# A new order for the prologue and the first two blocks of a planned kernel

## The chip, the cores and the metric

The kernel runs on one core of one Trainium2 chip. A core has five engines, each with its own queue that runs in order: TensorE (PE in the profile; PEld is its loading of weights), VectorE (DVE), ScalarE (ACT), GpSimd (POOL) and SyncE (SP), which here only issues transfers. An engine waits for another through semaphores. The metric is the time on the device in microseconds (us), the median of several runs. The profile shows one execution, with each instruction's start and duration.

## The reference

The reference carries `x` (128 sequences of 64 tokens, 256 features, fp32) through four layers, each added to its input. In short:

```python
# L0: style-modulated self-attention; q = k = v, 16 heads of 16
style = s @ aff_w.T + aff_b                       # one per sequence
w_mod = w[None] * style[:, None, :]
demod = rsqrt(sum(w_mod * w_mod, axis=2) + 1e-8)
kx    = einsum('bni,boi->bno', x, w_mod * demod[:, :, None]) + b
A     = softmax(einsum('bnhd,bnjd->bnhj', kx, kx) / 4)
x    += modulated_linear(einsum('bnhj,bnjd->bnhd', A, kx), s, o_aff_w, o_aff_b, o_w, o_b)
# L1: bottleneck, its weights made from the conditions
x    += x + relu(x @ (down * (c @ dg) + c @ db)) @ (up * (c @ ug) + c @ ub)
# L2: h, t, s are layer norms of x with gain and bias from tables;
#     m, n, r are x plus a small MLP of one condition each
cat   = concat([w0*h, w1*t, w2*m, w3*n, w4*r, w5*s])      # w = softmax(aw)
x    += layernorm(silu(cat @ W1 + b1) @ W2 + b2)
# L3: a weight matrix of rank 30 per sequence, decoded from mu
U     = (mu @ W_dec + b_dec).reshape(B, 257, 30)
x    += x @ (U[:, :256] @ V) + U[:, 256] @ V
```

## The kernel before

The 8,192 tokens are 16 blocks of 512 (8 sequences), each in 4 tiles of 128 tokens. A prologue makes what all blocks share. `prologue_keys` loads the weights of the attention and makes the styles and their demodulation: `style` (L512 on), `square` on GpSimd (L527 for the style, L528 for the weights), a product (L463), `root` (L535 adds, L536 takes the square root on ScalarE), a reciprocal (L544, L575), a store of `demod_k` to memory. `prologue_rest` makes the conditions of the other layers: `dgdb` and `ugub` by products with the conditions, stored and loaded again for each block; the softmax of `aw` (`wsm`, L599 to L603, whose exponential is L600); the scaled `int_W1` (L613, L620; GpSimd adds three of its parts to `w_x`, L624 and L625); `gtab` and `beta`, split into three bf16 terms by `terms_of` (L487 casts, L489 subtracts) and copied into place by ScalarE (L635, L655, L660); three small MLPs (L691 to L760); and 16 products by `W_dec` (`by_k`, L807, with VectorE's L812 behind each), stored as `ud`.

`attention` loads a block's inputs, has GpSimd multiply `xT` by the style (L900) and make the bottleneck's weights (`wdn` L931 and L937, `wup` L944 and L945), runs `tile_attention` for each tile, and ends with the output product (L957). One tile's attention is a chain over four engines: keys (L990), times demodulation (VectorE, L998), plus bias (GpSimd, L1004), a transpose (L1015), a copy `kR` (ScalarE, L1023), scores into the one `sc` buffer of four PSUM banks (L1046), maxima (VectorE, L1055, two), a copy of `mt` (ScalarE, L1065), a transpose (L1071), `mX` (ScalarE, L1078), `mTb` (VectorE, L1085), the shift by the maxima (L1096), exponentials (ScalarE, L1110, two), the product with the values (L1120), a transpose and a division (L1132 to L1139), a last transpose (L1150, L1155). The next scores need `sc` free, so they wait for the exponentials. `rest` runs the other layers of a block: down and up (L1178, L1196), layer norms (L1246 to L1276), the large product of the third layer (`int1`, L1314, fp32), the second (L1345), and the rank-30 product (L1388, L1414).

No loop sets the order of all this. Each operation is recorded in a `Plan` with its engine, an assumed duration, what it reads and writes and the buffers it needs; `Plan.order` then places the operations one after another. At each step it works out, for every operation that could be next, when it could start by these costs, and among those of an engine that can start within 0.02 us of the first it takes the one with the lowest turn number. The turn numbers are a table, `TURNS`: one list for the prologue, one each for the first and second block, one for the middle blocks, and one each for the last two; each block adds 400. The result is emitted in that order (`manual_schedule`), so the costs and numbers are only in the order, not in the program. Buffers go to operations in the same order, so another order also gives other buffer numbers.

What the costs of `order` know: TensorE's speed by windows of 3.41 us (full if the window before was busy for at least the share `BUSY`, by the weight `full` of each operation, and half otherwise); a switch of its tiling mode; SP's at most 8 transfers under way; and for operations with `pair=True`, VectorE operations that can't run beside a GpSimd one: such an operation starts only once GpSimd is free, and GpSimd's next only once it ends (`locked`).

Of the kernel before, what the change touches and what calls it, by code (L numbers as in the profile page):

```python
# [58 lines left out]
class Plan:  # L59
# [8 lines left out]
    LAG, WINDOW, BUSY, SEEN = 0.04, 3.41333, 0.4, 0.2  # L68
    TRANSFERS = 8
    SWITCH, KEEP = 0.08, 20.0  # L70
# [7 lines left out]
    def op(self, eng, took, emit, reads=(), writes=(), busy=None, claims=(), full=0.0, mode=0, pair=False, dma=0.0):  # L78
# [3 lines left out]
        o = dict(eng=eng, took=took, busy=took if busy is None else busy, emit=emit, full=full, mode=mode, pair=pair, dma=dma)  # L82
# [34 lines left out]
    def order(self):  # L117
# [18 lines left out]
        at, self.cells, landed, mode, locked, moved = {}, {}, [], 0, 0.0, 0.0  # L136
        ready = [o for o in ops if not o["wait"]]
        done = []
        while ready:
            best = {}  # L140
            for o in ready:
                pe = o["eng"] == "PE"
                other = at.get("POOL", 0.0) if o["pair"] else locked if o["eng"] == "POOL" else 0.0
                t = max([other, at.get(o["eng"], 0.0)] + [ops[d]["end"] + lag for d in o["deps"]] + [ops[d]["start"] for d in o["turn"]])
                need = {}
                for b in o["new"]:
                    need[b.kind] = n = need.get(b.kind, 0) + 1
                    free = self.free[b.kind]
                    if len(free) < n or (b.kind != "bank" and queue[b.kind][n - 1] is not b):
                        t = None  # L150
                        break
                    t = max(t, free[n - 1][0])
                if t is not None:
                    turn = o["prio"] - (self.KEEP if pe and bool(o["mode"]) == bool(mode) else 0.0)
                    best.setdefault(o["eng"], []).append((t, turn, o["n"]))
# [14 lines left out]
            if o["pair"]:  # L170
                locked = t + busy
            end = t + busy
# [29 lines left out]
    71 -14398 -26219 -39789 -3508 -7530 -8445 29350 -4645 -39544 -3719 31372 -23989 30872 -14104 -5225 32197 -4221  # L202
    -20468 16613 -32877 -15653 -20126 -4305 17337 6437 13955 1211 8610 -23732 17461 -40912 -33335 -37982 18051 10261
    200 -21211 -22777 -22750 -19011 -31532 -38047 -18609 7721 -34432 31396 -30213 -679 15634 -39760 15949 -34699
    42222 -32162 15768 -5238 -5839 -20496 -39810 -12031 32129 13701 32628 -5022 1049 17854 -28441 32340 -37891 -34297
    40989 -25748 -28541 36465 -17679 38337 -22124 -6381 -37871 18397 -22278 -45484 359 -1911 -29323 -49300 -46805
    4635 -91 19167 -31700 -47713 -3381 -5076 -40598 19254 -40704 18632 -38248 -38002 -13488 31826 -1701 18828 3175
    -34947 -15633 30124 -16980 57 31764 -8724 -42612 -38724 16630 18116 -23340 -3254 34040 -6466 -9239 -17832 33055
    -23773 14566 13689 29338 -5407 10846 18282 -1510 -48233 -30581 18938 -9903 -31147 21661 -7420 14038 17055 -42955
    -24882 -44299 -21176 -726 -25186 -4651 20657 -3370 30678 -10954 -12642 16581 -41643 -10283 17089 16935 -34492  # L210
    -21043 16515 -11836 16306 474 20673 5948 20829 15096 -17378 -4570 -24029 -14861 -3069 -28510 -6908 11872 21266
    -7806 -33448 -4644 8056 15322 -42611 20277 36585 -44360 -16351 17707 851 14726 16244 -34751 18196 38165 4440
    -13853 24639 -7896 11150 -5 -23772 15865 -46146 -35855 8441 32138 18178 -4413 -26345 -20553 14288 -39700 -47007
    10030 -4358 -34041 21308 -35652 17392 39213 13899 33152 -32620 15142 6721 14013 -35072 -14537 -1097 36082 -8009
    15339 34551 -34485 -1237 16822 -28641 -995 -30869 21364 16878 -14817 8219 -40040
    """,
    "first": """
    17249 -4174 -37661 40560 -2686 40232 13607 -21165 15661 -35071 -20748 8523 15848 9653 39437 -5504 -23078 -1003
    -23922 -12775 15184 21386 -5436 -38182 19015 -15238 17414 -6091 -41343 -14156 -19323 20301 -28060 25276 -38410
    -2885 8514 30733 -41166 16152 18629 10031 -32415 13671 6709 10311 35215 25762 -47432 6628 -14459 2665 -14344  # L220
    33918 17006 30738 -26444 -13871 5063 17282 -34231 16470 15297 -28168 -35683 -38013 -31479 885 -7241 -1609 -4616
    -35314 15778 11985 18356 16765 -13012 18386 -3827 -16703 27973 -35935 10508 16756 5142 -46417 5504 18379 -43542
    -36657 7698 34702 18688 18600 -8539 -6552 -43063 -6405 17215 7670 17794 -46636 -20647 -18240 29788 13458 -50498
    17553 -40018 -5173 19673 -30267 14660 3213 -4518 -35471 16525 7438 21762 -27033 17454 5856 -22658 -2548 -42968
    -1045 15141 -34414 -39228 -14781 -32852 -43405 37326 31094 -38278 -35006 17883 9658 -37158 15564 -38868 7399
    -45467 -810 -3547 329 -32846 -31322 21073 4944 -15877 -38629 42680 21792 -34201 -21934 27191 -15901 20512 -13401
    16412 -37057 16322 -44377 16841 27701 -19654 -45211 14418 17982 1404 -41845 16978 -6419 33218 -47006 34193 -25681
    18315 -8335 16994 -28170 43 18629 -3156 20131 9477 21282 21307 32185 16991 15525 4535 -26810 -36671 -3596 1849
    -43739 5277 -26259 31830 2526 -32783 -8029 -38301 21067 -6295 32999 -2430 -21725 333 -34823 -20585 13688 -13143
    -172 -33364 17594 16389 33686 -21070 -29862 -1422 30891 -7582 17309 -38340 1077 5561 -35769 19468 32463 -4083  # L230
    -628 16680 29479 -48232 -5761 -41402 5650 -34631 -43613 -42339 10399 -31952 -32906 29668 15652 13515 20461 -49991
    33105 34993 -35357 13650 -3425 -35040 -6276 17773 17502 19908 -34232 19985 20667 17372 -33978 13863 17147 16170
    -5010
    """,
    "second": """
    15875 16149 -15780 27079 -20038 -41412 -8527 31339 40458 -26784 -39981 -34505 -38008 -375 36397 -39093 23481
    17340 -7441 -37170 -1220 15851 -26304 -20057 16484 -24298 -9079 -48163 33051 -20470 33180 18143 16005 38721
    -21353 -42755 -3614 -4788 14775 16964 -7134 18850 -4650 13895 -18457 -12127 -3196 15705 16609 -6918 17201 16712
    -32722 -43102 2125 -36980 -4604 -39251 -25222 14438 18190 -28048 -3836 34949 -9979 -4441 -32439 3107 15923 -39292
    -32927 -3558 24709 -39978 35894 -1987 10347 -16156 -14048 12123 -39989 -47288 -29542 -31213 17510 12771 -39522  # L240
    -24706 17103 -6414 16875 22486 15550 -17008 14260 -37972 31898 -26161 164 -3567 -5559 -3644 -11986 -15142 -37679
    -47068 -2565 112 -47293 -2329 -35624 -30772 -35416 1153 -49693 -39768 14735 14656 32941 -6653 17076 29341 14823
    36957 -25310 35672 11924 20229 -23521 563 -19103 -28734 15957 8197 -3347 -31953 -40558 14704 -29232 17459 31147
    13855 -21768 14747 -40363 -30781 17758 34423 -14900 18160 813 20332 -5502 -27118 20085 27410 -21398 -50590 -26
    -3284 -8181 -3096 17263 -5282 15919 2531 -24344 -17581 -25179 16905 17897 13804 16385 33415 6275 -35571 15524
    -42367 -21853 28842 -5521 -15908 11063 -46061 -32321 -28271 14599 -169 4650 -27658 -31994 16439 -21317 -15239
    -27657 20557 -15331 30644 15572 37274 17208 -12718 -33262 -37729 -35554 4024 -28730 -40544 -17618 20660 39655
    -40762 -1182 18506 51 15653 -15776 34385 -51216 14294 -4243 -3255 -1485 -4941 -15608 -15247 -16446 -39940 13494
    -21568 16893 -29157 -7041 1652 -1804 -32667 32525 -12963 17265 -13279 236 6378 -43363 13245 6986 -46750 -41386
    -14016 40622 19379 -6583 -2003 -41355 -20538 -9037 13996 -11722 19545 -25139 -14909 11788 5525 -6727 -14631 16271  # L250
    -15192 -29513 -22936 17714 29105
# [53 lines left out]
def resid_chain(ctx: ExitStack, tc: tile.TileContext, a: dict, out: bass.AP, nblk: int = NBLK):  # L305
# [129 lines left out]
    def act(n, f, reads, writes, more=0.0):  # L435
        us = 0.085 + n / 1200 + more
        op("ACT", us + 0.08, f, reads, writes, busy=us)
# [20 lines left out]
    def product(us, ps, rows, cols, terms, reads, claims=()):  # L458
# [6 lines left out]
        pe(us, f, reads, [ps], claims)  # L465
# [16 lines left out]
    def terms_of(x, rows):  # L482

        out = []
        for t in range(TERMS):
            y = Buf("pb")
            dve(F, lambda y=y: nc.vector.tensor_copy(y.t[:rows], x.t[:rows]), [x], [y])  # L487
            if t < TERMS - 1:
                dve(F, lambda y=y: nc.vector.tensor_tensor(x.t[:rows], x.t[:rows], y.t[:rows], ALU.subtract), [x, y], [x])  # L489
# [3 lines left out]
    def prologue_keys():  # L493
# [37 lines left out]
        def root(dst, ps, n, part=None):  # L531
# [4 lines left out]
            act(n, lambda: nc.scalar.activation(view(), view(), AF.Sqrt), [d], [d])  # L536
# [1015 lines left out]
```

## Time and profile before

| | us |
|---|---|
| median of 3 runs | 910.79 (910.15 to 916.7) |
| the profiled execution, its time | 915.64 |
| its span, first to last instruction | 913.9 |
| TensorE busy | 835.8 (91%) |
| VectorE busy | 635.7 (70%) |
| GpSimd busy | 608.3 (67%) |
| ScalarE busy | 452.0 (49%) |

The page cuts the span into 40 slices; a digit is the busy share in tenths, and the row PEclk is the clock that TensorE was granted. The mean granted clock over the span is 0.967. By stretches, from the windows:

| stretch, us | TensorE busy | VectorE | ScalarE | GpSimd | clock |
|---|---|---|---|---|---|
| 0 to 130 | 98.0 | 87.8 | 53.3 | 71.8 | 0.87 |
| 130 to 210 | 76.4 | 53.2 | 35.9 | 44.7 | 1.00 |
| 210 to 860 | 626.8 | 478.6 | 349.2 | 473.9 | 1.00 |
| 860 to 913.9 | 34.6 | 16.2 | 13.6 | 18.0 | 0.75 |

Work of the prologue runs among the first two blocks until about 125 us; a block in the middle takes some 47 us. Within the first 130 us TensorE waited longest for:

| TensorE's waiting line | for | us, times |
|---|---|---|
| L463 | the load of `early` | 9.9, 1 |
| L1071 | ScalarE's copy of `mt`, L1065 | 5.3, 3 |
| L1046 | ScalarE's exponentials, L1110 | 2.4, 2 |
| L1150 | ScalarE's copy of `beta`, L655 (a bank) | 1.9, 1 |
| L1096 | VectorE's `mTb`, L1085 | 1.5, 2 |
| L463 | GpSimd's square of the style, L527 | 1.4, 1 |

### The profile page before, as it was taken

What the parts mean: (1) busy time and instruction counts of PE and PEld (TensorE: products, weight loads), DVE (VectorE), ACT (ScalarE), POOL (GpSimd) and SP (SyncE); (2) the same over time, 40 slices, a digit from 0 to 9 for tenths busy, and PEclk for the clock granted to TensorE, in tenths of its full rate; (3) what the DMA queues carried; (4) which work ended last, traced back from release to release, by engine and by line L of the source; (5) the groups of instructions that cost most, each with busy time, mean ns of one, the idle gap of its engine ahead of it and who ended that gap; (6) DMA issues with size and microseconds to landing.
All of it is one profiled execution on the core that took longest, in us unless ns stands there. A gap on an engine that the chain in (4) does not pass through costs nothing.

```text
span 913.9 us, 23971 instructions
## 1 busy us (share of the span) xinstructions
PE 835.8 (91%) x9752; PEld 538.6 (59%) x9752; DVE 635.7 (70%) x1363; ACT 452.0 (49%) x827; POOL 608.3 (67%) x826
## 2 busy tenths in 40 slices
PE   4768989899999999999999999999999999999793
PEld 3546855656575665656665756566566656564432
DVE  2667876758687777768585868777776858585532
ACT  2543254646455554555564655545554546454321
POOL 5265580967869594959687795959595968754513
PEclk9778999999999999999999999999999999999986
DMA  8466770242324232233324232323323232101000
GB/s 274 112 177 184 240 233 25 68 126 72 104 81 127 75 97 90 74 114 91 117 83 117 70 114 80 120 65 91 105 82 114 82 95 82 48 17 56 13 12 24
DMA packets 62575, 90.24 MB, mean 99 GB/s; under 512 B 6328, under 2 KB 46200, under 8 KB 62464
## 3 DMA queue, kind: packets, MB, share of 16 engines
q1 hardware_dynamic: 57344, 71.92, 26.9%
q0 software_dynamic: 5120, 16.78, 5.8%
q8 instruction: 77, 1.26, 0.6%
q14 instruction: 34, 0.28, 0.1%
HBM read 75.44 MB, written 13.24 MB: 97 GB/s over the span
## 4 chain that ended last, share of the span: by engine, by line
PE 71%; DVE 9%; ACT 6%; POOL 3%; issue 2%; POOLq 0%; ACTq 0%; DVEq 0%
PE bank L1314 22%; PE sc L1046 7%; PE bank L1120 6%; PE bank L957 6%; PE bank L1345 5%; PE bank L990 5%; DVE mt L1055 3%; PE bank L1033 3%; PE sc L1096 2%; PE bank L1150 2%; PE bank L1290 2%; ACT uu L1284 2%; PE bank L1178 2%; PE bank L1196 2%; PE bank L1371 2%
## 5 line engine op out<-in xcount | busy, mean ns | idle before, releaser
L1110 ACT ACTIVATE e<-sc 128x1024 f32<-128x1024 f32 x128 | 126.0, 1023 | 81.7 <-PE sc L1096 79.2
L1055 DVE TENSOR_REDUCE mt<-sc 128x8 f32<-128x1024 f32 x128 | 151.7, 1205 | 18.5 <-PE sc L1046 18.4
L1139 POOL TENSOR_TENSOR att<-ao,rz 128x256 f32<-128x256 f32 x45 | 28.3, 628 | 72.7 <-DVE rz L1136 66.7
L1299 DVE TENSOR_TENSOR uu<-uu,bank 128x512 f32<-128x512 f32 x96 | 63.9, 680 | 13.9 <-PE bank L1290 13.0
L990 PE MATMUL bank<-wk,xsT 128*128 128x256 f32 x256 | 68.4, 400 | 0.7 <-POOL xsT L900 0.7
L1314 PE MATMUL bank<-uu,w_t 128*128 128x512 f32 x128 | 66.4, 627 | 2.1 <-DVE uu L1299 1.4
L1314 PE MATMUL bank<-uu,w_s 128*128 128x512 f32 x128 | 67.2, 607 | 0.0
L1004 POOL TENSOR_TENSOR kxe<-kxe,kbr 128x256 f32<-128x256 f32 x64 | 46.8, 730 | 27.3 <-DVE kxe L998 27.2
L1314 PE MATMUL bank<-x2T,w_x 128*128 128x512 f32 x128 | 64.5, 605 | 0.0
L453 POOL TENSOR_SCALAR ry<-mvy 128x4 f32<-128x4 f32 (+1 forms) x19 | 4.4, 232 | 88.1 <-DVE mvy L449 87.9
L1345 PE MATMUL bank<-w,uu 128*128 128x256 f32 x256 | 61.7, 384 | 1.0 <-DVE uu L1332 1.0
L957 PE MATMUL bank<-osT,wo 128*128 128x512 f32 x128 | 60.9, 617 | 0.8 <-DVE osT L1155 0.7
L1046 PE MATMUL sc<-kR,kT 24*128 24x128 f32 x1440 | 58.0, 291 | 2.6 <-ACT e L1110 2.6
L1314 PE MATMUL bank<-uu,w_h 128*128 128x512 f32 x128 | 59.0, 595 | 0.1
L1046 PEld LDWEIGHTS sc<-kR,kT 24*128 24x128 f32 x1440 | 49.2, 193 | 16.3 <-issue 5.7
L990 PEld LDWEIGHTS bank<-wk,xsT 128*128 128x128 f32 x256 | 47.7, 198 | 17.2 <-issue 10.3
L931 POOL TENSOR_TENSOR wdn<-gdb,late 128x512 f32<-128x512 f32 x32 | 40.7, 1276 | 25.1 <-PE bank L1178 23.8
L448 DVE BATCH_NORM_STATS2 st<-uu 128x6 f32<-128x256 f32 x119 | 48.7, 418 | 9.3 <-ACT uu L1249 5.8
L1345 PEld LDWEIGHTS bank<-w,uu 128*128 128x128 f32 x256 | 46.2, 190 | 8.6 <-DVE uu L1332 1.6
L1132 DVE STREAM_TRANSPOSE ao<-bank 128x512 f32<-128x512 f32 x45 | 32.1, 713 | 26.5 <-PE bank L1120 23.2
L1065 ACT COPY mt<-mt 128x16 f32<-128x16 f32 x64 | 13.1, 204 | 74.3 <-DVE mt L1055 71.9
L915 POOL DMA_INDIRECT pw<-in_pw,idx x39 | 40.1, 1028 | 7.8 <-issue 7.0
(195 smaller groups left out, 2089.4 us busy)
## 6 DMA issues: line engine op xcount, KB each, us to landing
xT<-in_xT SPq DMA_DIRECT2D x32, 256.0 KB
gdb<-dgdb SPq DMA_DIRECT2D x16, 512.0 KB
wup<-ugub SPq DMA_DIRECT2D x32, 256.0 KB
ubb<-ugub SPq DMA_DIRECT2D x32, 256.0 KB
dmk<-demod_k SPq DMA_DIRECT2D x30, 256.0 KB
out_x<-uu SPq DMA_DIRECT2D x35, 128.0 KB
ud<-uu SPq DMA_DIRECT2D x8, 512.0 KB
uT<-ud SPq DMA_DIRECT2D x16, 256.0 KB
```

What stands on the lines that cost most here:

```text
L448: dve(256, lambda: nc.vector.bn_stats(st.t, x.t), [x], [st])
L931: lambda w=w, dp=dp: nc.gpsimd.tensor_tensor(w(), gdb.t[:, :, 0:64], dp, ALU.mult),
L957: nc.tensor.matmul(ps.t, owT[:, c, bass.ts(oc, 128)], osT.t[:, c, :], start=(c == 0), stop=(c == C - 1))
L990: nc.tensor.matmul(ps.t[:, :F], xsT.t[:, c, bass.ts(tl, 128)], kwT[:, c, :], start=(c == 0), stop=(c == C - 1))
L1004: lambda: nc.gpsimd.tensor_tensor(kxe.t[:, :, 0:D], kxe.t[:, :, 0:D], heads(kinds["kbr"][0]), ALU.add),
L1046: nc.tensor.matmul(sc.t[:, q, bass.ts(g, 128)], of_g(kT.t)[r, g, :], of_g(kR.t)[r, g, :], start=(g == 0), stop=(g == 3))
L1055: lambda two=two: nc.vector.tensor_reduce(mt.t[:, two, 0:4], sc.t[:, two, :].rearrange("p q (g n) -> p q g n", g=4), AX.X, ALU.max),
L1110: lambda k=k: nc.scalar.activation(es[k].t, sc.t[:, 2 * k : 2 * k + 2, :], AF.Exp, scale=0.25),
L1120: nc.tensor.matmul(ps_o.t[32 * q : 32 * q + 32, bass.ts(g, 128)], v.t.rearrange("p (g q d) -> p g q d", g=4, q=4)[:, g, q, :], es[q // 2]. ...
L1299: lambda ps=ps, src=src, dst=dst, c=c: nc.vector.tensor_tensor(dst.t[:, c, :], src.t[:, c, :], ps.t, ALU.mult),
L1314: lambda ps=ps, w=w, src=src, fc=fc, c=c, n=n: nc.tensor.matmul(ps.t, w.t[:, c, bass.ts(fc, 128)], src.t[:, c, :], start=(n == 0 and c == ...
L1345: nc.tensor.matmul(ps.t[:, :F], s2.t[:, c, bass.ts(tl, 128)], w2.t[:, c, :], start=(c == 0), stop=(c == C - 1))
```

## The change

It adds two things to what `order` counts, marks operations for them, and replaces three of the lists of turn numbers.

- A new cost: a ScalarE operation names the table set it needs (`table=1` for the square root, `table=2` for the exponential and the tanh; copies and scalings none). Where it differs from the set loaded last, the operation can start only 1.3 us after ScalarE is free.
- More VectorE operations are marked as unable to run beside GpSimd (`pair=True`): the casts and subtractions of `terms_of`, the scaling of `int_W1`, and three operations of the small MLPs.
- The products of the prologue count 0.7 of their time toward TensorE's activity, where they counted 1.0, and the share asked for is 0.43, where it was 0.4.
- The lists for prologue, first and second block are new. Those of the middle and last blocks are as they were.

```diff
-    LAG, WINDOW, BUSY, SEEN = 0.04, 3.41333, 0.4, 0.2
+    LAG, WINDOW, BUSY, SEEN = 0.04, 3.41333, 0.43, 0.2
     TRANSFERS = 8
+    TABLE = 1.3
...
-        at, self.cells, landed, mode, locked, moved = {}, {}, [], 0, 0.0, 0.0
+        at, self.cells, landed, mode, locked, moved, table = {}, {}, [], 0, 0.0, 0.0, 1
...
                 other = at.get("POOL", 0.0) if o["pair"] else locked if o["eng"] == "POOL" else 0.0
+                if o["table"] and o["table"] != table:
+                    other = at.get("ACT", 0.0) + self.TABLE
...
+            table = o["table"] or table
...
 TURNS = {
     "prologue": """
-    71 -14398 -26219 -39789 -3508 -7530 -8445 29350 -4645 -39544 -3719 31372 -23989 30872 -14104 -5225 32197 -4221
...
-        pe(us, f, reads, [ps], claims)
+        pe(us, f, reads, [ps], claims, full=0.7)
...
-            dve(F, lambda y=y: nc.vector.tensor_copy(y.t[:rows], x.t[:rows]), [x], [y])
+            dve(F, lambda y=y: nc.vector.tensor_copy(y.t[:rows], x.t[:rows]), [x], [y], pair=True)
...
-            act(n, lambda: nc.scalar.activation(view(), view(), AF.Sqrt), [d], [d])
+            act(n, lambda: nc.scalar.activation(view(), view(), AF.Sqrt), [d], [d], table=1)
...
-        act(6, lambda: nc.scalar.activation(w(0, 6), aw, AF.Exp, bias=w(6, 7)), [wsm], [wsm])
+        act(6, lambda: nc.scalar.activation(w(0, 6), aw, AF.Exp, bias=w(6, 7)), [wsm], [wsm], table=2)
```

What that does to the order can be read off the two built programs, engine by engine (lines are those of the kernel before):

- ScalarE: both square roots (L536) come ahead of the first exponential; the exponential of `wsm` (L600) comes just ahead of the first tile's (L1110). Four table loads become two: one at the very start, one ahead of L600.
- SP: `early` goes from 8th to 3rd, `int_W2` from 22nd to 4th, `late` from behind `xT` to 6th, `wk` from 3rd to 7th; the six loads of `int_W1` follow the store of `demod_k`, where five preceded it; the loads of `dmk` for the second and third block are apart.
- VectorE: the first tile's two maxima (L1055) have a mask comparison (L848) between them instead of a transpose and a key multiplication; the scaling of `int_W1` comes ahead of the second tile's maxima instead of behind them; of the terms of `gtab` and `beta`, nine instructions come ahead of the third tile's two maxima, where three came ahead of them and a fourth between them.
- GpSimd: the style's square comes ahead of the weights'; `xsT` ahead of the square of `wo`; `w_x` comes earlier, and the eight `wdn` instructions of the first two blocks nearly in one row, ahead of all of `wup`.
- TensorE: the same sequence up to the third tile but for small moves; then more `W_dec` products (L807) ahead of the first block's output product. From the third block's output product on, the order of all engines is the old one but for a few neighbours.

## The prediction

> **What bounds the kernel now.** I read the page's busy rows first, then the windows of the start, then the timelines of ScalarE, VectorE, GpSimd and TensorE between 0 and 130 us.
>
> ```profile
> span 913.9 us, 23971 instructions
> PE 835.8 (91%) x9752; PEld 538.6 (59%) x9752; DVE 635.7 (70%) x1363; ACT 452.0 (49%) x827; POOL 608.3 (67%) x826
> PE   4768989899999999999999999999999999999793
> PEclk9778999999999999999999999999999999999986
> ```
>
> TensorE is the bound: its digit is 9 nearly everywhere. Only the first five or six slices (22.8 us each) and the last four have lower digits, and only there the clock row drops. Windows of 0 to 130 and 130 to 210 us sum this up: TensorE is busy for 98.0 of the first 130 us at a mean granted clock of 0.87, and for 76.4 of the next 80 us at 1.00. So the first 130 us hold 32 us without work, of which 9.9 are the wait for the first load. In windows of 3.41 us (the steps in which the granted clock changes here), busy time times (1 - clock) sums to about 15 us. Some 47 us at most could be won ahead of 130 us, less whatever a start needs.
>
> The change moves only prologue and first blocks. From the third block's output product on (L957, at 208 us here) each engine's order is as it was but for a few neighbours. What is won or lost must arise before about 210 us; behind it a block costs what it cost.
>
> The windows around the worst hole:
>
> ```profile
> 51.20:54.61 3.41, 1.84 (x12) 1.26 (x10) 3.41 (x4) 1.21 (x3) 3.41 (x4) 1.00 0.93 210
> 54.61:58.03 3.42, 0.74 (x3) 0.34 (x3) 1.71 (x5) 2.28 (x7) 2.04 (x2) 0.95 1.08 240
> 58.03:61.44 3.41, 2.52 (x22) 1.90 (x23) 2.84 (x8) 1.74 (x5) 0.00 (x0) 0.50 0.84 255
> 61.44:64.85 3.41, 1.80 (x9) 1.24 (x11) 1.21 (x5) 3.35 (x8) 1.73 (x2) 0.50 0.00 0
> 64.85:68.27 3.42, 3.42 (x36) 2.88 (x37) 1.87 (x4) 0.61 (x1) 3.34 (x4) 0.50 0.02 5
> 68.27:71.68 3.41, 3.41 (x39) 2.19 (x39) 1.36 (x2) 0.51 (x2) 3.41 (x4) 0.55 0.26 79
> ```
>
> The columns are busy times of PE, PEld, DVE, ACT, POOL, then clock, DMA share and GB/s. TensorE has 2.6 us of work in 6.8 us, and then four windows are granted half the clock. VectorE is full in the first row with four instructions. Its timeline names them:
>
> ```profile
> 48.30 1.23 DVE L487 CAST pb<-p 96x256 bf16<-96x256 f32 x1 [0.51 <-DMA p<-in_gtab]
> 49.56 1.38 DVE L489 TENSOR_TENSOR p<-p,pb 96x256 f32<-96x256 f32 x1
> 50.97 1.24 DVE L487 CAST pb<-p 96x256 bf16<-96x256 f32 x1
> 52.14 1.21 DVE L1055 TENSOR_REDUCE mt<-sc 128x8 f32<-128x1024 f32 x1
> ```
>
> GpSimd's timeline, beside it:
>
> ```profile
> 48.12 2.54 POOL L931 TENSOR_TENSOR wdn<-gdb,late 128x512 f32<-128x512 f32 x2 [1.21 <-DMA gdb<-dgdb]
> 50.62 1.44 POOL L625 TENSOR_TENSOR w_x<-w_x,p 128x512 f32<-128x512 f32 x1
> ```
>
> Each of these VectorE operations has all operands in SBUF and ends 0.1 to 0.3 us behind a GpSimd instruction. Later the same cast takes 0.28 us (57.20) and the same subtraction 0.41 (53.27). That is the "hold". ScalarE's timeline shows the other cost that the old plan didn't know:
>
> ```profile
> 32.36 1.28 ACT L536 ACT_TABLE_LOAD   x1
> 33.65 0.51 ACT L536 ACTIVATE demod_o<-demod_o 128x128 f32<-128x128 f32 x2
> ...
> 39.10 1.28 ACT L600 ACT_TABLE_LOAD   x1
> 40.40 0.30 ACT L600 ACTIVATE wsm<-early,wsm 128x6 f32<-128x6 f32 x1
> 40.60 0.19 ACT L1065 COPY mt<-mt 128x16 f32<-128x16 f32 x1
> ```
>
> **The change part by part.** The plan's costs put no instruction into the program; they and the new turn numbers only reorder. The instructions are the same but for table loads: four in the old order, two in the new.
>
> *Start.* `early` (L495) goes from eighth on SP to third. It was issued at 4.00 us, and TensorE began at 9.89; the third place was issued at 1.65. So up to 2.35 us by issue, more if fewer bytes ahead count (160 KB instead of 1120): I bound it by 4.4. Against this, `late` (622 KB) and an `int_W2` load (256 KB) move ahead of `wk` and `xT`. `wk` then stands behind 1,509 KB including itself. The rows of the first windows moved 94, 179 and 370 GB/s, or 0.93 MB by 6.83 us, so those 1.55 MB are through at about 8.5 us; with 1.05 us for GpSimd's square of `wk` the first demodulation product (12.48 here) can begin near 10.5 us. `xT` of block 0 stands behind 2.4 MB, 10.8 us by the same rows, so the keys gain only about a microsecond and could lose one. The first key multiplication (18.68) waited for the demodulation. Taken: 1.6 us; ends -1 and 4.4. Also on SP, the six `int_W1` loads go behind the store of `demod_k`, where five were ahead of it; they are multiplied from 42.37 us on, so even 15 us less leaves them time: nothing. The four `dmk` loads that hold SP from 21.79 to 28.18 are split two and two, with `down_gb`, `in_small`, `up_gamma`, the store of `dgdb` and `mem_W2` between, so `gdb` and with it GpSimd's `wdn` can begin some microseconds earlier; who waits for it is only block 0's down product (97.3): nothing.
>
> *Two table loads.* The load at 32.36 holds the roots of `demod_o`, which hold the reciprocals, which in VectorE's queue hold the maxima of the second tile (35.67), whose scores ended at 34.4: 1.28 us of path. The load at 39.10 holds the copy of `mt`, ready at 39.35 and done from 40.60: 1.25. Together 2.5 us. A rule speaks for more: the Trainium skill, ScalarE: Activation LUTs, section What ACT_TABLE_LOAD costs, gives 1.28 us for the load and about as much again for a drain, 2.66 for a switch. Two switches would be 5.3. Here the work behind a load begins 0.01 to 0.02 us after it and the load 0.02 after what is ahead; the row decides: 2.5. If TensorE has other work there: 1.3. The remaining load stays just ahead of the first exponentials, as now.
>
> *Second tile.* The first tile's maxima (24.72 to 28.01) have a transpose and a key multiplication between them, 1.0 us; in the new order a mask comparison of 0.47. Gain 0.6.
>
> *Third tile.* Its scores end at 48.18, its maxima begin at 52.14 behind held casts, end at 54.81; `mX` starts at 58.14 behind three `gtab` copies, one of `beta` and two of `tab`, though its transpose ended at 55.44. Five casts and subtractions took 5.05 us against 1.66 by their free durations: 3.4 us of hold. In the new order ScalarE has two `tab` copies (0.71) between, which gives about 1.7 us. But the maxima now stand behind all of the `gtab` terms and four of `beta`'s five (nine instructions, 3.0 us unheld), and GpSimd's eight `wdn` instructions follow one another near there, so the hold is not gone by order alone. I take half of it, 1.7. Sum 3.4; ends -4 and 6.
>
> *Clock.* The half-clock windows from 58.03 hold 11.15 us of busy time: 5.4 us lost. A rule bears on it: the Trainium skill, TensorE: Matmul & The Clock Gate, section What's actually happening, says that one busy window of about 3.4 us restores the full clock. By that only the first of these windows is lost, 1.3 us. The rows deny it: 64.85 to 68.27 is busy throughout, and the next window is still at 0.55. I go by the rows, and as the hole shrinks by about half, take 2.5; ends 0 and 5.4.
>
> *Later holds.* L700 took 1.30 at 81.70 and 1.21 at 98.61 instead of 0.28: 2 us of VectorE. TensorE is at 10.0 of 10 us from 90 to 110, which hides the second. Taken 0.6.
>
> *At nothing.* `w_x` and `wdn` earlier on GpSimd (idle from 56.7 to 63.1); more `W_dec` products ahead of block 0's output product (same work, TensorE full there); `cseq` stored later (its `tab` is read some 15 us of TensorE work later). Where that cover goes, the wait would be two landings, some 5 us.
>
> Sum: 1.6 + 2.5 + 0.6 + 3.4 + 2.5 + 0.6 = 11.2 us. The profiled execution took 915.64 (span 913.9), so it would be 904.4; the median shown is 910.79, 4.85 lower, and gives 899.6.
>
> **The rivals.**
>
> *Given back (0.24).* From 80 to 130 us VectorE is busy 43.5 of 50 us and TensorE is full from 90 to 110. An attention that runs earlier may only wait there. Then start and table loads survive, about 4 us: 907. For it: VectorE's work is the same. Against it: VectorE was free for 5.8 of 10.2 us from 61.4 to 71.7, and TensorE for 32 us.
>
> *Slower (0.07).* The third tile's maxima stand behind nine casts and subtractions in one queue, and `beta`'s wait in turn for nine `gtab` copies on ScalarE (0.41 each, 3.7). If each of the nine is held by a GpSimd instruction of 1.27, they take 11.4 us; with the copies the maxima come about 15 us after the scores instead of 4, and three half-clock windows cost 1.5 each. That is 11 + 4.5 against gains of 4.7 at start, loads and second tile: about +11, 922. It decides once the maxima begin more than 9 us after the scores.
>
> *It does not do what it says (0.05).* The holds stay and only the loads go: 908.3.
>
> **How the numbers follow.** My forecast has 0.64 and 890 to 903 as its own range. About 1%, 9.1 us, is what a measurement of this kernel can tell from no change. Faster by more: 0.62. Within: 0.02 of my forecast, 0.24 and 0.05, so 0.31. Slower: 0.07. The range for 8 in 10 runs from 890 (start and clock at their good ends) to 908.5, which takes in the given-back case and leaves the slower one out.
>
> **What would show it.** First matmul near 6 to 8 us; two ACT_TABLE_LOAD instead of four, none between 30 and 45; the third tile's shift (L1096, 59.96) about 7 to 9 us earlier; no run of four half-clock windows; the third block's output product (208) 11 us earlier, and equal distances behind. I am wrong if casts still take 1.2 us ahead of the maxima, or if the lead at the third tile is gone by block 0's output product (88.9).

## The result, and the profile after

The changed kernel takes 897.11 us (median of 5 runs, 896.84 to 898.11), the kernel before on the same chip 910.79 (5 runs, 908.17 to 916.7). The ratio is 0.9845, with a 95% interval of 0.9808 to 0.9881: 13.7 us faster, where 11.2 were forecast. The time came out near the forecast; most of the places did not. Medians and mean clocks are of fast runs alone (two of the 19 of the kernel before in the first set below, at 926.5 us, are left out as slow).

The page of the changed kernel, with the lines that answer to those shown of before:

```profile
span 895.1 us, 23962 instructions
PE 824.6 (92%) x9752; PEld 534.3 (60%) x9752; DVE 635.5 (71%) x1363; ACT 446.8 (50%) x825; POOL 608.0 (68%) x826
PE   5769999999999999999999999999999999999783
PEclk9889999999999999999999999999999999999996
```

TensorE's busy row stays at 9 from the fourth slice on, where it did from the seventh, and its clock row from the fourth instead of the fifth. The windows of the changed kernel by stretch (busy time of PE, PEld, DVE, ACT, POOL, then clock, DMA share, GB/s):

```profile
0.00:130.00 130.00, 104.43 (x1066) 74.88 (x1067) 93.29 (x180) 52.49 (x106) 77.16 (x99) 0.95 0.71 206
130.00:215.00 85.00, 80.64 (x1059) 52.46 (x1059) 60.09 (x133) 44.38 (x83) 54.16 (x76) 1.00 0.33 88
```

Before, the first row had 98.0 us of TensorE at a clock of 0.87. Both clocks are too high, and so is every mean clock here: the clock column prints 1.00 from the start, but the trace's list of clock changes begins only where TensorE first gets the full clock. That is at 16.7 us in the profile of before, at 26.8 in that of the changed kernel, and at 18.3 in its second one. Ahead of that point matmuls take the time of half clock. A window of the first profile after, and the same four products in the first and in the second:

```profile
17.07:20.48 3.41, 3.41 (x8) 1.86 (x7) 1.04 (x2) 0.37 (x1) 0.81 (x1) 1.00 0.81 256
18.60 2.07 PE L466 MATMUL bank<-p,p 8*128 8x256 f32 x4
```

```profile
18.64 1.13 PE L466 MATMUL bank<-p,p 8*128 8x256 f32 x4
```

So the sums below count one half ahead of the first full clock. They split what TensorE lost into time without work ("idle") and time at half clock (busy time times one minus the clock), in us. The last column is the same changed program, profiled a second time:

| stretch, us | before: idle, clock | after: idle, clock | after, second time |
|---|---|---|---|
| 0 to 17.07 | 11.3, 2.7 | 11.1, 3.0 | 11.5, 2.8 |
| 17.07 to 71.68 | 13.3, 13.0 | 12.8, 10.2 | 13.1, 7.5 |
| 71.68 to 129.71 | 7.4, 1.7 | 1.6, 0.0 | 1.5, 0.0 |
| sum | 32.0, 17.4 | 25.6, 13.2 | 26.1, 10.3 |

So the waits ahead of 72 us gave hardly anything (24.6 us of idle time before, 24.0 and 24.6 after). The clock ahead of 72 us gave 2.5 us in the first profile after and 5.4 in the second. The largest part, 7.5 us, comes from 72 to 130 us: 5.8 of idle time and 1.7 of clock. (The prediction's "about 15 us" of half clock before is 17.4 with the start.)

The two profiled spans differ by 18.8 us, more than the medians. Of this, 12.8 us are there at the third block's output product. Most of the rest is not the new order: from there to the 16th block's output product the profile of before took 639.2 us and that of after 635.5, but `maxima_ahead_before` below, with the old order, took 635.0 beside 635.6 of the changed kernel in the same set. In the last 60 us the clock cost 6.8 us in the profile of before, 2.4 in that of after and 6.6 in its second one.

The moments that the prediction named, from the timelines:

| us | before | after | after, second time |
|---|---|---|---|
| first matmul | 9.89 | 4.01 | 4.19 |
| first demodulation product | 12.48 | 11.69 | 12.20 |
| first key multiplication (VectorE) | 18.68 | 20.26 | 19.77 |
| shift of tiles 1, 2 | 29.55, 42.16 | 32.23, 42.85 | 30.42, 41.10 |
| shift of tiles 3, 4 | 59.96, 74.45 | 60.90, 72.39 | 59.31, 70.76 |
| last `W_dec` products | 114.3 | 103.0 | 101.5 |
| first products with `int_W1` | 128.55 | 115.32 | 113.80 |
| third block's output product | 208.03 | 195.21 | 195.09 |

The third tile's shift is not 7 to 9 us earlier but 0.9 us later (0.7 earlier in the second profile). The windows around the hole ahead of it, after:

```profile
54.61:58.03 3.42, 0.74 (x3) 0.34 (x3) 3.39 (x7) 0.51 (x2) 3.42 (x4) 0.92 1.10 228
58.03:61.44 3.41, 1.59 (x20) 1.06 (x20) 2.99 (x6) 1.82 (x5) 3.41 (x4) 0.50 0.51 163
61.44:64.85 3.41, 3.41 (x17) 3.05 (x14) 1.57 (x3) 2.76 (x4) 1.78 (x3) 0.58 0.03 12
64.85:68.27 3.42, 3.42 (x71) 2.60 (x71) 3.23 (x6) 0.00 (x0) 2.49 (x3) 1.00 0.52 142
```

The hole is no smaller: 0.74 us of work in the first window, 1.59 in the second (0.74 and 2.52 before). What has changed is what follows: two windows near half clock instead of four. VectorE's timeline shows why the hole stayed:

```profile
45.16 1.20 DVE L490 CAST pb<-p 96x256 bf16<-96x256 f32 x1 [2.36 <-DMA p<-in_gtab]
46.62 1.15 DVE L492 TENSOR_TENSOR p<-p,pb 96x256 f32<-96x256 f32 x1
...
52.37 0.28 DVE L490 CAST pb<-p 32x256 bf16<-32x256 f32 x1 [2.78 <-ACT p L660]
...
53.79 1.21 DVE L1062 TENSOR_REDUCE mt<-sc 128x8 f32<-128x1024 f32 x1
```

The five casts and subtractions of `gtab` take 4.06 us (1.20 + 1.15 + 0.70 + 0.72 + 0.29), against 5.05 before and 1.66 free: the hold is still there. GpSimd's timeline, beside them:

```profile
42.51 2.48 POOL L938 TENSOR_TENSOR wdn<-gdb,late 128x512 f32<-128x512 f32 x2 [0.85 <-DMA gdb<-dgdb]
44.95 2.53 POOL L944 TENSOR_TENSOR wdn<-wdn,gdb 128x512 f32<-128x512 f32 x2
```

The four `wdn` instructions end at 47.5 us, and until then each cast and subtraction ends 0.1 to 0.3 us behind one of them. The first of them waited 2.36 us for `gtab`, and `beta`'s first cast 2.78 for ScalarE's copy of `beta`; the maxima stand behind both, 1.65 us later than before (52.14). Behind them the shift waits again: `beta`'s last cast takes 1.35 us (57.50) instead of 0.28. On ScalarE `mX` (59.62) stands behind the copies that wait for it, though its transpose ended at 57.0. And TensorE waits 2.29 us for a bank that VectorE's L819 empties only behind that cast.

### The profile page after: what moved, and what is told of

Same layout as the page of the kernel before. It is cut to its first block, busy times and chain, and to the rows that moved or that the text cites. A ratio compares the mean times of both kernels' runs of the same rounds, so it can differ in the third digit from the quotient of the medians.

```text
span 895.1 us, 23962 instructions
## 1 busy us (share of the span) xinstructions
PE 824.6 (92%) x9752; PEld 534.3 (60%) x9752; DVE 635.5 (71%) x1363; ACT 446.8 (50%) x825; POOL 608.0 (68%) x826
## 4 chain that ended last, share of the span: by engine, by line
PE 44%; POOL 26%; DVE 13%; issue 6%; ACT 6%; DMA 3%; SPq 1%; POOLq 0%; DVEq 0%; ACTq 0%
PE bank L1322 15%; PE sc L1053 4%; DVE mt L1062 4%; PE bank L964 3%; PE bank L1353 3%; PE bank L1128 3%; PE bank L997 3%; POOL kxe L1011 2%; POOL wdn L938 2%; POOL uu L1271 2%; DVE st L451 2%; POOL xsT L907 2%; POOL uu L1265 2%; ACT uu L1240 2%; POOL uu L1364 1%
## 5 line engine op out<-in xcount | busy, mean ns | idle before, releaser
L1322 PE MATMUL bank<-uu,w_t 128*128 128x512 f32 x128 | 63.2, 604 | 2.2 <-DVE uu L1307 2.2
L1072 ACT COPY mt<-mt 128x16 f32<-128x16 f32 x64 | 13.1, 204 | 84.0 <-DVE mt L1062 83.9
L1005 DVE TENSOR_TENSOR kxe<-bank,dmk 128x256 f32<-128x256 f32 x64 | 26.8, 419 | 29.9 <-PE bank L997 26.8
L952 POOL TENSOR_TENSOR wup<-wup,ubb 128x512 f32<-128x512 f32 x32 | 40.6, 1269 | 3.5 <-DMA ubb<-ugub 1.3
```

Source lines behind the costliest of these rows:

```text
L952: pool(1.25, lambda w=w: nc.gpsimd.tensor_tensor(w(wup), w(wup), w(ubb), ALU.add), [wup, ubb], [wup])
L1322: lambda ps=ps, w=w, src=src, fc=fc, c=c, n=n: nc.tensor.matmul(ps.t, w.t[:, c, bass.ts(fc, 128)], src.t[:, c, :], start=(n == 0 and c == ...
```

## The experiments

Every kernel is timed against the kernel before on its own chip, whose median was 919.14 us in the first set of four, 912.65 in the second and 921.37 in the third; compare ratios. The changed kernel unaltered was timed again in the second set alone; against the other sets its 0.983 or 0.9845 is a comparison across chips. An interval of 0.004 to 0.005 either way is some 4 us. In the diffs, `put(x, a, b)` moves operations a and b of the finished order directly ahead of x; an operation is named by its block (-1 is the prologue) and its number in it. The expectations name four theories. "Path": the prediction's sum. "Clock": most of the gain is fewer half-clock windows. "Filler", formed after the first set: real work put into TensorE's waits gives the gain, and a lead of the tile's chain alone is lost at the next wait. "Activity", formed after the second: the clock of a window depends on how much of the array worked in the one before it.

**The changed kernel again** (`after_again`, no edit).

> The changed kernel unaltered, on the same chip as the runs beside it, as their yardstick. Both theories: 0.981 to 0.988 of before.

Measured: 897.49 us, 0.983 [0.98, 0.9859]. The yardstick holds.

**The third tile's step alone, on the kernel before** (`maxima_ahead_before`). 79 and 80 are `gtab`'s first cast and subtraction, 84 and 83 the third tile's maxima, 85 to 89 its copy, transpose, `mX`, `mTb` and shift.

```diff
     done = plan.order()
+    put((-1, 79), (0, 84), (0, 83), (0, 85))
+    put((-1, 80), (-1, 94), (0, 86), (0, 87), (0, 88))
+    put((-1, 110), (0, 89))
```

> The kernel before with the third tile's step alone put right: its maxima go ahead of the three gtab casts on VectorE, its maxima copy and mX ahead of the gtab copies on ScalarE, its transpose ahead of a W_dec product and its shift ahead of a small product on TensorE. The third tile's shift (59.96 us) should come 5 to 7 us earlier. Theory 'path': that is the larger part of the forecast (3.4 and 2.5 of clock), so 4 to 7 us faster than before, ratio 0.992 to 0.996. Theory 'filler' (the tile chain is not what bounds here; the gain is from real work that keeps TensorE busy through its waits, and the chain's lead is lost again at the next wait): within 2 us of before.

Measured: 0.9992 [0.9975, 1.0009] over 22 runs, no difference. TensorE's timeline of this kernel:

```profile
54.29 0.40 PE L1096 MATMUL sc<-mTb,sel 8*128 8x128 bf16 x16
54.81 0.80 PE L463 MATMUL bank<-early,p 128*128 128x128 f32 x2
57.48 0.66 PE L1150 MATMUL bank<-ident,att 128*128 128x128 f32 x2 [1.88 <-ACT p L655]
59.76 1.12 PE L1033 MATMUL bank<-ident,kT 128*128 128x128 f32 x4 [1.61 <-DVE uu L812]
...
65.44 2.09 PE L1046 MATMUL sc<-kR,kT 24*128 24x128 f32 x32 [2.43 <-ACT e L1110]
```

The shift comes at 54.29, 5.7 us earlier, and the lead is gone eleven microseconds on. TensorE waits 1.88 us for a bank that ScalarE's copy of `beta` has to empty, and the third tile's exponentials run at 61.97 and 64.36 us where they ran at 61.15 and 63.54: in ScalarE's queue they stand behind the copies of the tables and of `v`. The fourth tile's shift is at 75.09 (before 74.45). The two small tables and the banks bound this stretch, not the maxima.

**The same step on the changed kernel** (`maxima_ahead`): the third tile's maxima and copy ahead of `beta`'s terms, its `mX` ahead of their copies.

```diff
+    put((-1, 96), (0, 83), (0, 84), (0, 85))
+    put((0, 88), (-1, 101), (-1, 102), (-1, 103), (-1, 104), (-1, 106), (-1, 105))
```

> The changed kernel with the third tile's maxima ahead of four casts and subtractions of beta, and its copy and mX ahead of the beta copies on ScalarE. The third tile's shift (60.90 us) should come 2 to 3 us earlier. Theory 'path': 2 to 4 us faster than the changed kernel, and with one half-clock window less perhaps 5. Theory 'filler': less than 1.5 us either way.

Measured: 894.93 us, 0.9808 [0.9774, 0.9841], 2.6 us below the unaltered one beside it by the medians, with intervals that overlap. The shift came 1.6 us earlier than in that one (57.69, 59.31), and by 61.44 us TensorE had lost 0.7 us less to holes and clock together.

**The start** (`late_behind`): `int_W2`, `sel` and `late` behind the first block's `xT` on SP, the product that reads `late` between the key products.

```diff
+    put((1, 0), (-1, 76), (-1, 4), (-1, 7))
+    put((0, 52), (-1, 184))
+    put((-1, 62), (-1, 185), (-1, 77))
```

> The changed kernel with the loads of int_W2, sel and late behind the first block's xT on SP, and the product that reads late between the first two key products. The first demodulation product (11.69 us) should begin near 9 us and the first key multiplication (20.26) 1.5 to 2.5 us earlier. Theory 'path': 1.5 to 2.5 us faster than the changed kernel. Theory 'filler': the lead is kept only as far as TensorE has work at once, 0 to 1.5.

Measured: 897.14 us, 0.983 [0.9798, 0.9862], 0.35 us from the unaltered one. The demodulation product begins at 8.75 us instead of 11.69 (first profile of the changed kernel), and by 13.65 us TensorE has done 5.0 us of work instead of 3.0 in the yardstick. The next waits (1.04 for `xsT`, 1.10 for `late`, 0.55 for `seqs`) take most of it back: the third tile's shift is at 60.19. (This run got its first full clock at 26.4 us, its yardstick at 18.3, so single moments of the two differ by that too.)

**Two table loads put back into the changed kernel** (`tables_back`). `behind` appends a one-column activation to an operation: here to the first tile's second exponential and to a copy ahead of the second tile's maxima copy.

```diff
+    behind(0, 45, AF.Sqrt)
+    behind(-1, 51, AF.Exp)
```

> The changed kernel with two more table loads on ScalarE, at the places where the old order had them: a one-column Sqrt behind the first tile's exponentials and a one-column Exp just ahead of the second tile's maxima copy. Theory 'path': 2.5 us slower than the changed kernel (1.3 if TensorE had other work), near 899.5. Theory 'clock': ScalarE has slack at the first of them, and TensorE other work at both: less than 1 us slower, below 898.

Measured: 0.9803 [0.9755, 0.9851], no slower than the changed kernel's 0.983 to 0.9845 by the points; 2 us could hide in the intervals. The trace says more. ScalarE's timeline:

```profile
36.81 1.28 ACT L1449 ACT_TABLE_LOAD   x1
...
39.29 1.28 ACT L1449 ACT_TABLE_LOAD   x1
40.59 0.20 ACT L1449 ACTIVATE scr<-scr 128x1 f32<-128x1 f32 x1
41.47 0.20 ACT L1072 COPY mt<-mt 128x16 f32<-128x16 f32 x1 [0.68 <-DVE mt L1062]
```

ScalarE still waits 0.68 us for VectorE's maxima behind the second load; without the loads it waited 3.71. From first to second shift it is 10.73 us with them and 10.62 without.

**The counting alone** (`counted_old_lists`): the new costs with the old turn numbers.

> The new costs (table loads, the hold, the weight of products in the clock) with the old turn numbers: the new counting alone. It has two table loads, as the changed kernel. If the counting carries the gain ('path', whose two terms of loads and holds it counts), 900 to 905. If the new turn numbers carry it by what they put ahead on TensorE ('clock'), 906 to 915.

Measured: 1057.4 us, 1.1469 [1.141, 1.1527]. Neither theory foresaw it. Turn numbers mean something only beside the costs they were searched with; this run says nothing of what a counted cost is worth.

**Idle waits filled with dummy work** (`warm_before`, `warm_after`): transposes of the identity ahead of operations that wait, into the bank that they then overwrite.

```diff
+            for _ in range(n):
+                nc.tensor.transpose(ps.t[:, :128], ident, ident)
             real()
```

> The kernel before, with 18 transposes of the identity put ahead of four TensorE operations that wait there (6 ahead of the second tile's maxima transpose at 40.85 us, 4 ahead of the third's at 55.11, 5 ahead of the attention transpose at 57.32, 3 ahead of the transpose of kT at 58.91). No other instruction moves. Theory 'clock' (most of the gain is that TensorE runs fewer windows at half its clock): the half-clock windows at 41 to 48 and 58 to 72 us shrink, 4 to 6 us faster than before, near 906. Theory 'path' (the prediction's sum: start, table loads and holds on the tile's chain, clock only 2.5): 0 to 2.5 us faster, or 1 to 2 slower where the transposes overrun the wait.

> The changed kernel, with 20 transposes of the identity in its own three longest waits of the tiles (5 ahead of the first tile's maxima transpose at 31.08 us, 9 ahead of the third's at 56.67, 6 ahead of the transpose of kT at 59.85). Theory 'clock': the half-clock windows at 34 to 41 and 58 to 65 us, which lose 5.2 us, go at least in part: 2 to 5 us faster than the changed kernel, 892 to 895. Theory 'path': 897, within 1 us, or 1 us slower.

Measured: 0.9997 [0.9964, 1.003] and 0.9827 [0.9779, 0.9876], no difference from the kernel before and from the changed one. The mean clock over the runs rose from 0.9625 to 0.9693 in the first, and by 71.68 us the profiled run had lost 10.4 us to the clock instead of 15.7. But by 92 us it had been idle for 1.8 us more, and the 18 transposes hold TensorE for 3.1 us; the dummies cost about what the clock gave. A full clock bought with work that nobody needs is no gain.

**The rows of the array** (`rows_before`): the four products of `demod_k` over 128 rows instead of 8, the other rows zeros; the time of the matmuls themselves is the same.

```diff
-                lambda tl=tl: [(seqs0.t[:NB, bass.ts(tl, 128)], dk.t[:NB, :])],
+                lambda tl=tl: [(seqs0.t[:, bass.ts(tl, 128)], dk.t)],
...
+        nc.vector.memset(seqs, 0.0)
```

> The kernel before with its four products of demod_k (8 rows of the array in use, 4.1 us of TensorE) run over 128 rows, 120 of them zeros: the same matmuls with the same columns, one memset more at the start. In the trace of before, TensorE is busy for 0.90 of the window ahead of 20.15 us, two thirds of it with these products, and the next window has half the clock. Theory 'activity' (what sets the next window's clock is how much of the array works, not how long TensorE is busy): no half-clock window at 20 to 24 us, and the lead of about 1.6 us shows at the first tile's scores (23.46 us). Theory 'busy time': the same half-clock window stays, and nothing moves. The whole time is within 2 us of before by both.

Measured: 0.996 [0.9937, 0.9984] over 22 runs, 3.7 us faster by the ratio, more than either theory gave. The mean clock rose from 0.9625 to 0.968. First the windows of the kernel before around its first drop, then those of this kernel from its own first full clock on (17.43 us):

```profile
16.73:20.15 3.42, 3.08 (x19) 1.58 (x18) 1.41 (x4) 1.40 (x4) 0.73 (x1) 1.00 1.00 301
20.15:23.56 3.41, 2.85 (x12) 2.03 (x12) 1.91 (x4) 2.30 (x4) 0.90 (x1) 0.50 0.65 189
```

```profile
17.43:20.84 3.41, 2.52 (x18) 1.37 (x11) 1.62 (x4) 1.69 (x5) 0.73 (x1) 1.00 0.93 293
20.84:24.26 3.42, 3.42 (x45) 2.81 (x45) 2.39 (x5) 1.92 (x3) 1.83 (x3) 1.00 0.58 141
```

TensorE is busy for 3.08 us of the first window in the kernel before, and the next window has half the clock. With 128 rows it is busy for less, 2.52 us, and the next window has the full one. The same products in TensorE's two timelines:

```profile
17.54 2.29 PE L463 MATMUL bank<-p,p 8*128 8x256 f32 x8
```

```profile
17.49 2.30 PE L463 MATMUL bank<-p,p 128*128 128x256 f32 x8
```

The lead of 1.4 us at the first shift (28.19) has grown to 3.0 at the third (56.97), and by 51.2 us the clock had cost 6.8 us instead of 10.3; 2.8 are left at the first `int_W1` product (125.75).

One pair of profiles would not be enough, because the windows begin elsewhere in each run. In the profile of `warm_before`, whose program is that of before up to its first dummies (36.69 us), the windows begin at 15.2 and 18.6 us and split the eight products, and neither is followed by half clock. It is the 22 runs against 27 that carry the result.

**Combinations** on the changed kernel: `both` is `maxima_ahead` and `late_behind`; `both_tabs` adds the line below (loads of `gtab` and `tabT` earlier); `both_rows` is `both` with the 128 rows.

```diff
+    put((-1, 140), (-1, 78), (-1, 93))
```

> The changed kernel with maxima_ahead and late_behind together. Taken one by one they gave 2.6 and 0.35 us. Theory 'path': 3 us faster than the changed kernel, near 894.5. Theory 'filler': up to 4, since the start's lead is real TensorE work that is through before the hole at 54 us, if the hole is shorter too: 893.

> As the run before it, with the loads of gtab and tabT two W2 loads and a store earlier on SP. TensorE waited 2.0 us for tabT at 45 us and VectorE 2.4 for gtab. Both theories: the wait at 45 us falls below 1 us; 'path' 1 to 2 us faster than without, 'filler' 0 to 1, as the window at 44 to 48 us is at full clock already.

> The changed kernel with maxima_ahead and late_behind and the demod_k products over 128 rows. Theory 'activity': no half-clock window ahead of 30 us in any phase of the windows, up to 1.7 us faster than without the rows where one had been, with less spread. Theory 'busy time': no difference.

Measured: 0.9833 [0.9788, 0.9878], 0.9782 [0.9736, 0.9828] and 0.981 [0.9765, 0.9854]. `both` shows no gain over the changed kernel, where the theories gave 3 and up to 4 us; its interval does not exclude them. Windows of its profiled run:

```profile
17.07:20.48 3.41, 3.41 (x10) 2.08 (x8) 2.15 (x5) 0.87 (x3) 1.04 (x2) 0.50 1.00 360
20.48:23.89 3.41, 3.41 (x13) 2.28 (x16) 1.21 (x3) 1.05 (x3) 1.34 (x2) 0.50 1.12 211
23.89:27.31 3.42, 3.42 (x36) 2.92 (x37) 1.48 (x2) 1.19 (x2) 0.25 (x1) 0.50 0.14 25
```

TensorE never pauses for three windows and never leaves half clock: the 8-row products (16.62 to 20.8 us with one style product between), a key product and the transpose of `kT`, and then the 24-row scores (23.68, 2.09 us) fill them. In `both_rows` the window from 18.67 to 22.09, which 128-row matmuls fill, is followed by the full clock.

That did not decide the time. By 30.72 us half clock had cost 9.2 us in `both` and 6.1 in `both_rows`, which got its first full clock only at 22.1 us; "no half-clock window ahead of 30 us" did not come true. In `both_tabs` it had cost 10.5, as the first full clock came at 30.4, and that kernel has the lowest ratio of all. It lies 4 to 6 us under the changed kernel's and 4.7 under `both`'s by the points, where the theories gave 0 to 2 over `both`, and its wait for `tabT` is gone. Its interval still overlaps the changed kernel's in the second set (0.98 to 0.9859): it beats the kernel before, and that it beats the changed one is not shown.

## Why the prediction was right in its time and wrong in its places

The sum of 11.2 us was near the 13.7 by luck. The four terms for waits ahead of 72 us, 8.1 us together, came to 0.6 us of idle time in one profile and to nothing in the other. The terms for what follows, 0.6 and "at nothing", came to 7.5. The clock ahead of 72 us gave 2.5 and 5.4, where 2.5 were forecast.

- **Start, 1.6: wrong.** `early` landed even sooner than forecast (first matmul at 4.01). But TensorE then waited 3.9 us for `late`, and 2.25 more for GpSimd's square of `wk`, which began when `wk` landed, at 10.60 us. The step had `wk` through at about 8.5, once the 1.55 MB up to it in order of issue had moved. By 10.60 us the windows of the changed kernel (83, 257, 300 and 352 GB/s) had moved 2.3 MB, so transfers issued later moved beside it. By 17.07 us both kernels had lost the same (14.0 and 14.1 us). `late_behind` showed that even 2.9 us at the demodulation product come to 0.35 at the end.
- **Two table loads, 2.5: present in part.** Two loads are left (0.73 and 32.73). First to second shift took 10.62 us instead of 12.61 (10.68 in the second profile). But the remaining load did not stay as it was. Before, it ran ahead of the shift's end, and the exponentials began 0.4 us behind that; now it stands behind the roots of `demod_o` and two copies, and they begin 1.8 us behind it. The step counted the removal and not the move. That also puts the load at 32.73, inside the 30 to 45 us where its sign wanted none. In the new order a load costs nothing where ScalarE waits anyway (`tables_back`).
- **Second tile, 0.6:** part of the same 2 us; not measured by itself.
- **Third tile, 3.4: wrong.** Its sign "wrong if casts still take 1.2 us ahead of the maxima" came true. Half the hold was guessed to go; 1.0 of 3.4 us went, and the waits for `gtab` and for the copy of `beta` took its place. The other half, 1.7 us for `mX`, did not come either: it runs 2.6 us behind the end of its transpose, 2.7 before. And `maxima_ahead_before` shows that in the old order the step, done alone, is worth nothing.
- **Clock, 2.5: about the right size, for another reason, and not all of it.** From 57.5 to 72 us, where the forecast looked, half clock cost 5.4 us before and 2.3 and 2.2 after. It was to shrink with the hole; the hole didn't shrink, the run of half-clock windows did. Another 3.1 us were won at 41 to 48 us (3.1 lost before, none after), where the forecast didn't look. Against this stands the start, printed as 1.00: up to 26.8 us half clock cost 4.1 us before, and 7.8 and 5.1 after. What TensorE runs in a window has a part in this; that is shown at 20 us alone (`rows_before`), not behind 40. In the prediction the Trainium skill (TensorE: Matmul & The Clock Gate, What's actually happening) was weighed: one busy window of about 3.4 us restores the full clock. By it the first three of the four windows would have been lost, not the first alone, since the third was the first one busy throughout. The rows of `both` deny it more plainly than that of before: three windows busy throughout, all at 0.50.
- **Later holds, 0.6, and "at nothing": too small.** From 71.68 to 129.71 us idle time fell from 7.4 to 1.6 us, by 2.4 ahead of 90 us and by 3.8 behind 110. Here the order has more to do: 92 of the 120 matmuls of `W_dec` run ahead of the first block's output product, where 48 did. They end 11 us sooner (103.0), and the first block's `int_W1` products begin 13 us sooner. The step that put this at nothing ("same work, TensorE full there") named the cover at 90 to 110 us and didn't ask what stood empty on either side of it (from 110 to 130 TensorE had 15.84 of 20 us of work before, 19.67 after). That this move is the cause is read from the two traces; no run moved these products alone, so the largest part of the gain is argued and not shown.

Of the rivals, "given back" came true for the start, and in `maxima_ahead_before` for the third tile: such leads were lost at the next wait. In the changed kernel the third tile had no lead to lose, and the first block's output product comes 2.0 us later (90.94; 0.5 later in the second profile), behind more `W_dec` products; the time was won elsewhere. The slower one didn't: the third tile's maxima stood behind nine casts, 3 us behind the end of its scores and not 9.

## What to carry to other kernels

Before crediting a wait that goes, ask what the operation behind it waits for next, in every queue that it passes through: a shift 5.7 us earlier was worth nothing here. Before reading a clock row of a start, compare the durations of equal matmuls there and later: a row of 1.00 covered matmuls at half clock for the first 13 to 30 us. Where TensorE's clock drops, look at which matmuls fill the windows ahead of the drop, and try more rows for those of few; here that was worth 0.4% in the kernel before, and nothing certain on top of the changed one. Dummy work in the waits raised the clock and cost the same time.

## What the runs showed of the hardware

- The clock granted to TensorE followed how much of its array was in use, not only how long it was busy: 3.08 busy us of 3.41 with mostly 8-row products led to 0.50 in the next window, 2.52 with 128 rows to 1.00. Half clock can last through windows without a pause (three in `both`).
- TensorE began each profiled run at half clock, by its matmuls (0.43 us from one fp32 product of 256 columns to the next, 0.22 behind the first full clock), and first got the full one between 13.3 us (`both`) and 30.4 us (`both_tabs`). The same program got it at 26.8 us in one profile and at 18.3 in another.
- Where the windows begin against the kernel differs from run to run, and with it which of them drop. The changed kernel's second profile has a drop at 21.7 us; its first, still at half clock until 26.8, has none there. Over 27 runs of the kernel before in the second set the span went from 903.4 to 913.9 us and the mean clock from 0.975 to 0.957, the longer spans mostly with the lower clocks (correlation -0.87).
